# Four-layer network on one core: in the last layer, the three units that issue two pairs of projection pieces move one unit forward

## The chip, the core and the metric

The kernel runs on one core of a Trainium2 chip. The metric is device time in microseconds of one execution. TensorE (PE) multiplies matrices, VectorE (DVE) and GpSimd (POOL) work element by element, ScalarE (ACT) evaluates functions and copies, SyncE (SP) issues most DMAs. Each engine takes its own instructions strictly in order, so a wait at the head of a queue holds everything behind it.

## The reference, cut to what matters

Four layers run one after the other on a tensor of 2 x 192 x 96 x 96. Each is `x = x + layer(groupnorm(x))`. Only the fourth is touched, a selective state-space scan (Mamba) over the 9216 places of an image:

```python
xz = x_flat @ W_in.T                      # 192 -> 768, split into x_in and z_gate
xc = causal depthwise convolution of x_in, 4 taps, + conv_b
x_conv = silu(xc)
x_dbl = einsum('bdl,kd->blk', x_conv, W_x)   # dt (12), B (16), C (16)
delta = softplus(dt @ W_dt.T + 2 * b_dt)
h = exp(delta * A) * h + (delta * x_conv) * B    # 384 channels x 16 states, step by step
y = (h . C + D * x_conv) * silu(z_gate)
out = y @ W_out.T
```

## The kernel before, in words

**Steps and units.** `layer3` cuts the two images into 38 steps of up to 511 places (two short ones of 265 and 264 at the start and at the end). The 6144 pairs of channel and state of a step lie in 12 units, q = 0 to 11, of 4 x 128 rows. A unit k does this:

- PE spreads delta over the rows into four banks of PSUM (`steps_of`, L2466), ACT takes their exponential in place (`decay`, L2480), POOL multiplies the loaded input by B (`times_b`, L2456, tile `bu`), DVE runs four scans (`scan`, L2489, tile `h`).
- DVE multiplies three quarters of h by C (`times_c`, L2513, tile `hc`), POOL the last quarter (`times_c_aside`, L2524, tile `hp`), and PE sums over the states (`sum_of`, L2537, tile `acc`; every fourth unit begins with the skip term, L2531). Every fourth unit DVE gates the sum (`gate`, L2550, tile `y`).
- SP loads the `bu` tile of unit k + 3 (L2441, 1 MB), into one of four buffers.

**Pieces beside the units.** Three generators are run piece by piece between the units' own instructions. `output` (L2562, L2570) projects the finished step before this one. `late` (L2380 to L2430) makes delta for the next step; its last pieces are three POOL operations, `ln`, `dl` and `du` (L2421, L2423, L2425), and four DMAs that write `du` out as `ud` (L2427), from which the `bu` loads of the next step read. `early` prepares the step after the next. After two pieces on ACT (copy of the tail, normalization `xn`) it yields after each of these:

- six projections, P0 to P5: two matmuls on PE (L2344), then one copy on ACT, into `xi` for P0 to P2 (L2352; after P2 also a small copy of the tail, L2354) and into `zs` for P3 to P5 (L2359);
- three convolutions, C0 to C2: four matmuls on PE (L2364), then one bias operation on ACT into `us` (L2368);
- the two silu operations on ACT (L2370, L2371).

The PE half and the ACT half are separate pieces: one call of `go("early")` issues one half. All of these results, and those of `late` and `output`, go through one bank of PSUM, `pe`, which exists once: a projection's first matmul waits until the ACT half of the pair before it has read the bank.

**Who orders what.** PE, ACT, DVE and POOL follow the program order written by hand (`manual_schedule`); SP is not in that list, so the order of its DMAs is the planner's. Within unit k the program order of what matters here is: the pair of `AHEAD[q]`, both halves at once; `sum_of(k - 2)`; `scan(k)`; `steps_of(k + 1)`; the PE half of the pair of `BEHIND[q]`; `decay(k + 1)`; the ACT half of that pair; `times_c(k)`; the gate; the POOL operations; two small ACT copies (`start_of`, L2449, and `keep`, L2496). An AHEAD pair thus stands on PE ahead of the unit's sums and of the next unit's spreading, and its ACT half ahead of the next unit's exponentials; a BEHIND pair stands behind both.

Before the change the pairs of `early` are issued as follows (A for AHEAD, B for BEHIND):

| unit q | 5 | 6 | 7 | 8 | 9 | 10 |
|---|---|---|---|---|---|---|
| pairs | P0 (B) | P1 (B) | P2 (A), P3 (B) | P4 (A), P5 (B) | C0 (A), C1 (B) | C2 (B) |

Of the kernel before, what the change touches and what calls it, by code (L numbers as in the profile page):

```python
# [63 lines left out]
class Net:  # L64
# [2113 lines left out]
    def layer3(self, x, out, stats):  # L2178
# [13 lines left out]
        with ExitStack() as ctx:  # L2192
# [283 lines left out]
            def decay(k):  # L2476
                s, q, _, _ = where(k)
                for r in range(4):
                    da = got[s]["da", q][r][:, 1:]
                    nc.scalar.activation(  # L2480
                        da, da, AF.Exp, scale=nA[:, 4 * q + r : 4 * q + r + 1]
                    )
# [103 lines left out]
            rows_c(0)  # L2586
            steps_of(0)
            decay(0)
            AHEAD = {1: "late", 7: "early", 8: "early", 9: "early"}
            BEHIND = {  # L2590
                0: "late",
                1: "late",
# [12 lines left out]
            def go(name):  # L2605
                next(running[name], None)

            for k in range(nk):
# [5 lines left out]
                if q == 3 and s + 2 < ns:  # L2614
                    running["early"] = early(s + 2)
                if q in AHEAD:
                    go(AHEAD[q])
                    go(AHEAD[q])
                if k >= 2:
# [137 lines left out]
```

## Time and profile before

| | |
|---|---|
| median of 3 runs | 10140.82 us (10130.94 to 10147.6) |
| the profiled execution's own time | 10135.06 us |
| its span, first to last instruction | 10133.3 us |
| scans of the last layer | 7009.5 to 10122.1 us of the span |
| a full step of the last layer | 85.0 us on the mean from scan to scan, twelve units |
| PE / DVE / POOL / ACT busy over the span | 89% / 82% / 69% / 60% |

A full step is read from the timeline: the time from the first scan of one step to the first scan of the next, for steps 3 to 33. Busy shares say little about the order inside a step; the chain of waits and the timeline of one step do. "Granted clock" is the share of full speed that the throttle gave TensorE; its records change at multiples of 3.41 us and hold 1.0 or 0.5. A line such as `7536.29 1.98 PE pe L2344 x4` of the chain view reads: at 7536.29 us of the span the chain lay for 1.98 us on PE, on matmuls of line 2344 writing tile `pe`, four of them (each f32 matmul is recorded as two passes).

### The profile page before, as it was taken

How to read it: one execution, taken by the hardware profiler on the slowest of the kernel's cores; microseconds unless marked ns; L12 is line 12 of the kernel's file. 1: busy time of each engine (PE TensorE's matmuls, PEld its weight loads, DVE VectorE, ACT ScalarE, POOL GpSimd, SP SyncE). 2: the span in 40 equal slices, each digit the busy share in tenths (PEclk: the TensorE clock that was granted, in tenths of full speed). 3: DMA queues.
4: the chain of work that ended last, by engine and by line, in shares of the span. 5: the costliest groups of instructions: out<-in, count | busy, mean ns of one | idle time of the engine just before them, and what ended most of it. 6: DMA issues, size and time to landing. Idle time of an engine off the chain costs nothing. (4 is left out here: it accounts for less than half of the span.)

```text
span 10133.3 us, 222497 instructions
## 1 busy us (share of the span) xinstructions
PE 9017.0 (89%) x87686; PEld 5301.1 (52%) x87686; DVE 8276.5 (82%) x8874; ACT 6078.5 (60%) x11850; POOL 7002.5 (69%) x5653
## 2 busy tenths in 40 slices
PE   4799999999979999999979777787999999999998
PEld 3578878877768877788853222223222222222223
DVE  5788878888768887777756789885899999999998
ACT  0366666666657766677721169664666666666665
POOL 1466676666666666666630258774899999999998
PEclk8899999999989999999989888987999999999998
DMA  8455555555424455455545344443788878788876
GB/s 147 96 135 136 140 135 138 136 136 135 126 72 136 137 144 143 138 137 139 137 117 159 122 141 164 125 128 80 173 178 180 178 178 180 178 178 176 180 177 150
DMA packets 878318, 1465.18 MB, mean 145 GB/s; under 512 B 251745, under 2 KB 682405, under 8 KB 877189
## 3 DMA queue, kind: packets, MB, share of 16 engines
q1 hardware_dynamic: 663276, 1264.09, 49.1%
q0 software_dynamic: 105152, 133.19, 5.7%
q10 hardware_dynamic: 108840, 53.57, 2.1%
q8 instruction: 701, 11.49, 0.5%
q14 instruction: 349, 2.85, 0.1%
HBM read 871.06 MB, written 381.46 MB: 124 GB/s over the span
## 5 line engine op out<-in xcount | busy, mean ns | idle before, releaser
L616 DVE TENSOR_TENSOR sp<-h 128x2304 f32<-128x2304 f32 x790 | 2183.5, 2796 | 34.4 <-ACT h L595 34.4
L2489 DVE TENSOR_TENSOR_SCAN h<-da,bu 128x512 f32<-128x512 f32 (+2 forms) x1824 | 1981.2, 1147 | 239.7 <-ACT da L2480 189.7
L2456 POOL TENSOR_TENSOR bu<-bu,bs 128x2044 f32<-128x2044 f32 (+2 forms) x456 | 1960.0, 4298 | 175.9 <-DMA bu<-ud 127.9
L640 ACT COPY st<-pt 128x512 f32<-128x512 f32 (+1 forms) x2370 | 1214.0, 515 | 1090.0 <-PE pt L632 1017.8
L632 PE MATMUL pt<-ident,sp 128*128 128x128 f32 x14220 | 1677.0, 276 | 84.0 <-DVE sp L616 39.0
L638 DVE COPY st<-pt 128x512 f32<-128x512 f32 x1580 | 1060.3, 687 | 760.2 <-PE pt L632 748.4
L632 PEld LDWEIGHTS pt<-ident,sp 128*128 128x128 f32 x14220 | 1567.9, 142 | 166.1 <-issue 95.5
L586 POOL TENSOR_TENSOR h<-u,step 128x1152 f32<-128x1152 f32 (+1 forms) x474 | 1106.9, 2354 | 628.5 <-DVE u L559 436.9
L604 POOL DMA_DIRECT2D xw<-xp_d x2500 | 1391.0, 619 | 153.9 <-PE pt L683 53.4
L2480 ACT ACTIVATE da<-da,nA 128x511 f32<-128x511 f32 (+2 forms) x1824 | 1063.6, 639 | 583.2 <-PE da L2466 577.2
L683 PE MATMUL pt<-st,xw 64*32 64x288 f32 (+1 forms) x30000 | 1107.7, 370 | 169.1 <-DVE st L638 92.1
L709 ACT COPY val<-pt 128x288 f32<-128x288 f32 (+1 forms) x3000 | 958.7, 404 | 306.3 <-PE pt L683 285.6
L811 PEld LDWEIGHTS pf<-main,wd 126*64 126x64 f32 x17064 | 913.9, 140 | 155.6 <-issue 148.4
L811 PE MATMUL pf<-main,wd 126*64 126x128 f32 (+1 forms) x17064 | 986.5, 274 | 9.6 <-DMA far_m<-val 9.2
L2466 PE MATMUL da<-dl,spread 32*128 32x511 f32 (+2 forms) x3648 | 888.2, 650 | 17.5 <-DVE h L2489 17.4
L683 PEld LDWEIGHTS pt<-st,xw 64*32 64x32 f32 x30000 | 547.7, 106 | 594.7 <-DVE st L638 167.6
L2513 DVE TENSOR_TENSOR hc<-h,cc 128x1533 f32<-128x1533 f32 (+2 forms) x456 | 750.7, 1646 | 0.0
L832 PE MATMUL pf<-more,wl 118*64 118x144 f32 (+5 forms) x11592 | 732.9, 277 | 2.5 <-DMA more<-far_l 2.4
L832 PEld LDWEIGHTS pf<-more,wl 118*64 118x64 f32 (+1 forms) x11592 | 665.7, 137 | 69.7 <-issue 62.7
L2466 PEld LDWEIGHTS da<-dl,spread 32*128 32x128 f32 x3648 | 281.2, 194 | 599.7 <-DVE h L2489 370.2
L2524 POOL TENSOR_TENSOR hp<-h,cs 128x511 f32<-128x511 f32 (+2 forms) x456 | 552.7, 1212 | 47.5 <-DVE h L2489 35.6
L2344 PE MATMUL pe<-xn,sb_w_in 96*128 96x511 f32 (+2 forms) x864 | 479.7, 683 | 91.5 <-ACT zs L2359 38.7
(360 smaller groups left out, 13089.2 us busy)
## 6 DMA issues: line engine op xcount, KB each, us to landing
bu<-ud SPq DMA_DIRECT2D x408, 1022.0 KB
main<-val SPq DMA_DIRECT2D x2016, 91.1 KB
far_l<-val SPq DMA_DIRECT2D x288, 324.0 KB
xw<-xp_d POOLq DMA_DIRECT2D x2500, 26.0 KB, 3.1
far_m<-val SPq DMA_DIRECT2D x288, 162.0 KB
half_d<-hv SPq DMA_DIRECT2D x54, 768.0 KB
hv<-half_d SPq DMA_DIRECT2D x54, 768.0 KB
more<-far_l SPq DMA_DIRECT2D x576, 60.8 KB
```

What stands on the lines that cost most here:

```text
L586: nc.gpsimd.tensor_tensor(hs, u[:, :, 8 * KK * l : 8 * KK * l + n].unsqueeze(3).to_broadcast([P, 2, n, WS]), con["step"].unsqueeze(1).unsq ...
L604: nc.gpsimd.dma_start(out=xw[e * WN : (e + 1) * WN, i], in_=xp_d[y : y + WS, x : x + WS, e * CM // 2 : e * CM // 2 + XW],)
L616: nc.vector.tensor_tensor(sp.rearrange("p s (y x) -> p s y x", x=WS), hy.unsqueeze(3).to_broadcast([P, n, WS, WS]), hx.unsqueeze(2).to_bro ...
L632: nc.tensor.transpose(pt[:, q], sp[:, 2 * (q0 + q) : 2 * (q0 + q) + 2].rearrange("p e w -> p (e w)"), self.ident,)
L640: nc.scalar.copy(st[:, q0 : q0 + m], pt[:, :m])
L683: nc.tensor.matmul(to, xw[e * WN : (e + 1) * WN, win, g * CG : g * CG + 32], sts[pair][e * WN : (e + 1) * WN].rearrange("p s (r c) -> p s ...
L811: nc.tensor.matmul(place(cv, m, 2 - t // 3, 2 - t % 3, None, 0), con["wd"][:, cv, t, m * CO : (m + 1) * CO], blocks(took, 1, rows), start= ...
L832: nc.tensor.matmul(place(cv, m, 2 * cv if alone else 1 - cv, 2 - t, h, 1 - alone,), con["wl"][lanes, slot, t, m * CO : (m + 1) * CO], bloc ...
L2456: nc.gpsimd.tensor_tensor(bu, bu, got[s]["bs"].unsqueeze(1).to_broadcast([P, 4, steps[s][2]]), ALU.mult)
L2466: nc.tensor.matmul(das[r][:, 1:], spread[at, v].rearrange("p n e -> p (n e)"), got[s]["dl"][at, i], start=True, stop=True, tile_position=( ...
L2480: nc.scalar.activation(da, da, AF.Exp, scale=nA[:, 4 * q + r : 4 * q + r + 1])
L2489: nc.vector.tensor_tensor_scan(h[:, r], got[s]["da", q][r], bu[:, r], 0.0, ALU.mult, ALU.add)
```

## The change

The three units whose `AHEAD` entry is "early" become q = 6, 7, 8 instead of 7, 8, 9. `BEHIND` stays as it is.

```diff
-            AHEAD = {1: "late", 7: "early", 8: "early", 9: "early"}
+            AHEAD = {1: "late", 6: "early", 7: "early", 8: "early"}
             BEHIND = {
                 0: "late",
                 1: "late",
```

The pairs of `early` come in the same order as before, so the table becomes:

| unit q | 5 | 6 | 7 | 8 | 9 | 10 |
|---|---|---|---|---|---|---|
| pairs | P0 (B) | P1 (A), P2 (B) | P3 (A), P4 (B) | P5 (A), C0 (B) | C1 (B) | C2 (B) |

P1 to P5 and C0 change their place in the queues of PE and ACT; P0, C1, C2 and the silu operations stay where they were. `early` issues one DMA, the load of `xt`, in its first piece at q = 3, which is not moved. No instruction is added or removed.

## The prediction

> **What bounds the kernel now.** I read the slices of the page first, then the chain of waits over one full step, then the timeline and the stretches of the same step. The page says where the last layer lies and that four resources are nearly full in it:
>
> ```profile
> PE   4799999999979999999979777787999999999998
> DVE  5788878888768887777756789885899999999998
> POOL 1466676666666666666630258774899999999998
> PEclk8899999999989999999989888987999999999998
> DMA  8455555555424455455545344443788878788876
> ```
>
> From slice 28 on (the last layer, 3113 us, 38 steps) nothing is idle enough to tell, so the order inside a step decides. The chain of waits of the step that begins at 7485 us, from unit 6's scan being prepared to the end of unit 9:
>
> ```profile
> 7525.85 3.70 PE pe L2344 x4
> 7529.55 1.70 PE acc L2531 x2
> 7531.25 0.99 PE acc L2537 x8
> 7532.25 1.11 PE da L2466 x8
> 7533.35 2.37 ACT da L2480 x4
> 7535.72 0.52 ACT xi L2352
> 7536.25 0.04 issue
> 7536.29 1.98 PE pe L2344 x4
> ...
> 7547.39 2.37 ACT da L2480 x4
> 7549.76 0.53 ACT zs L2359
> 7550.29 0.04 issue
> 7550.33 3.70 PE pe L2364 x8
> 7554.03 0.99 PE acc L2537 x8
> 7555.02 1.07 PE da L2466 x8
> 7556.09 3.63 PE pe L2364 x8
> ```
>
> The reader sees no DVE and no POOL in it: from 7525.85 until the silu operations at 7570.75 this step's chain is PE and ACT. Three times it crosses over: da on PE, four exponentials on ACT (2.37), the ACT copy of the BEHIND pair (0.52), and back to PE for the AHEAD pair, which waited for that copy because bank `pe` exists once. The first crossing leads to P2, the second (7540.37) to P4, the third (7547.39) to C0. P1, P3 and P5 lie under the exponentials and cost the chain nothing. One full crossing unit is 7532.25 to 7539.27 = 7.02 us; DVE needs 6.13 for a unit (the shortest distance of two scans in the timeline).
>
> P0 and the skip take twice the 1.91 and 0.86 us that such work takes later in the chain. The stretches tell why:
>
> ```profile
> 7525.80:7529.60 3.80, 3.75 (x4) 1.15 (x4) 0.50 0.68 186
> 7609.62:7613.04 3.42, 2.75 (x4) 1.17 (x4) 3.42 (x5) 0.66 (x1) 3.42 (x1) 0.50 0.51 131
> 7613.04:7616.45 3.41, 3.41 (x8) 0.87 (x10) 3.41 (x4) 0.77 (x3) 3.41 (x2) 0.50 0.86 223
> ```
>
> The granted clock (the third number from the end) is 0.50 when P0 runs, and so it is in unit 5 of each of the 30 full steps I looked at. In the second row, the same place a step later, PE was busy 2.75 of 3.42 us and the clock stayed at half; after the third, busy throughout, it came back at 7616.45. In the last layer no half-clock stretch of 3.41 us with 0.6 us or more of idle PE ended in a full clock.
>
> **The change part by part.**
>
> P1 moves ahead of unit 6's sums. On PE it now follows P0 directly, and must wait for P0's ACT copy (0.58 us at 7529.64 in the timeline, after P0's last pass at 7529.55) to free the bank: P1 begins at 7530.30, 0.75 us after P0's end. Queued behind it on PE are the skip, the sums and the spreading for unit 7; unit 7's exponentials and scan wait for those. Before, P1 was free. So the chain gains 0.75 + P1. At full clock P1, skip and sums are 1.91 + 0.86 + 0.99 = 3.76 us.
>
> The clock: the 0.75 us hole falls into the 3.41 us stretch that before was solid PE work and brought the clock back (here 7527.70 to 7531.11). With 78% busy it is like the row of 2.75 in 3.42, and I take it that it does not bring it back. Then the next solid stretch begins 0 to 3.41 us after P1's start, and full clock comes 3.41 to 6.82 us after it, 5.12 on the mean. Half of 5.12, 2.56 us of work, is done by then, the other 1.20 follow: da of unit 7 begins 6.32 us after P1's start (bounds 5.46 and 7.17), at 7536.62 instead of 7532.25, that is 4.37 us late (3.51 to 5.22).
>
> C0 leaves the third crossing. After da of unit 7 the chain has two crossings of 7.02 (to P3 and to P5), then 1.07 + 3.70 (C0, now behind the spreading) + 0.99 + 1.07 to C1: 20.87 us, where before 7532.25 to 7556.09 were 23.84. That gives back 2.97 us. From C1 on nothing differs.
>
> Net, with the clock held back: +4.37 - 2.97 = **+1.40 us a step** (+0.54 to +2.25). In 5 of the 30 steps the clock is already back when P0 ends (8.8 to 9.0 us after unit 5's scan); there P1 runs at full speed and the net is 0.75 + 1.91 - 2.97 = -0.31. Mean: 25/30 x 1.40 - 5/30 x 0.31 = +1.12.
>
> Nothing absorbs it on the usual step: unit 12's exponentials, then both silu on ACT, then unit 13's exponentials make the next link, and DVE is idle before unit 13's scan by 1.09 us on the mean, so a late ACT delays it in full. DVE itself is never ahead again: from da of unit 7 it needs about 41.0 us to the scan of unit 13 (1.9 + 7.02 + 7.02 + 6.72 with the gate + 3 x 6.13), ACT 45.1 - 2.97 = 42.1. But in 4 of 29 steps POOL waited so long for its `bu` (DMA, L2441) that unit 11's scan was later than the delayed one would be; those lose nothing: x 0.85, +0.95.
>
> Edits of no cost: the ACT copies of P1 to P5 stay one per unit and side; `start_of(9)` comes at about 20.3 us after unit 5's scan instead of 15.9, and POOL needs it at 22.6 (cover 2.3 us; if gone, `times_b(9)` slips by the rest, and unit 9's scan, due at 32, has still 5 us). The POOL chain from `ln` to `times_b(9)` starts at DVE's L2419 and stays. SP: no DMA moves; the loads of units 13 to 15 wait for scans that are 1 to 4 us later, bounds 0 and 1 us a step, I take 0 as each lands a unit ahead.
>
> Some 33 steps count (36 run `early`, the short ones count half): 33 x 0.95 = 31 us on the profiled execution's own 10135.06: 10166. That execution lies 5.8 us under the median of 10140.82; against the median I predict 10172.
>
> The Trainium skill speaks the other way on the hole: "TensorE: Matmul & The Clock Gate", section "HAM oscillation", names PE idle gaps above about 3.4 us as what costs the clock. By that, 0.75 us would be harmless and each step would go by the -0.31. The row of 2.75 in 3.42 decides for me.
>
> **Rivals.**
>
> *The clock comes back in spite of the hole*, at P0 and P1 of unit 6, so that P1 runs full. It decides if 0.75 us idle of 3.41 suffices. For it: stretches with only 0.2 to 0.3 us of idle did both. Against: the 0.6 us row above. Price: 33 x -0.31 = -10 us, 10131: not slower.
>
> *The planner puts the load of unit 10 ahead of the first `ud` write.* Now SP issues it at 7542.40, behind the write at 7542.01, though its buffer was free at 7532.4; POOL then idles 1.5 to 3.5 us before `times_b(10)`. For it: in the first three steps the order is another. Against: 30 steps alike, and unit 6's scan does not move. If so, unit 11's late POOL goes too, some 0.5 us a step: with the full clock -27 us, 10114.
>
> *POOL and DMA hide more*: unit 11's scan waits 0.3 to 0.5 us behind `times_b(11)` in the median step; if DMA were later by 1 us, only a third of the delay would show, +10 us, 10151.
>
> *Loads late*: if units 13 to 15 do slip by 1 us, +33 more, 10205.
>
> **How the numbers follow.** This kernel can be told from no change at about 0.2%, 20 us. Forecast (+15 to +63: the bounds of the net x 0.85 x 33): 0.68; clock back: 0.13; planner: 0.05; hidden: 0.08; loads late: 0.06. A little of the forecast lies under +20. Slower 0.70, same 0.22, faster 0.08. The range: from the clock-back case shared over half the steps (10140) to 1.8 us in each of 33 steps (10200).
>
> **What would show it.** Right: in unit 6 P1 takes 3.7 us at clock 0.50; unit 6's scan to unit 7's is about 10 us (6.41 before), unit 9's to unit 10's 6.7 (8.61 before); one crossing fewer in the chain; the full clock some 3 us later than before. Wrong: P1 of 2 us in most steps, a chain through POOL `bu`, or another order of `bu<-ud` and `ud<-du` on SP.

## The result, and the profile after

The kernel after the change took 10205.28 us (median of 4 runs, 10197.38 to 10209.64), beside 10139.06 us of the kernel before: a ratio of 1.0062 (95% interval 1.005 to 1.0073). Beside runs of before in two later sessions it measured 1.0047 (1.0032 to 1.0062) and 1.0050 (1.0037 to 1.0063). It is slower, as forecast, but by some 50 to 66 us where 31 were forecast, and 10205 lies outside the range of 10140 to 10200.

The profiled execution took 10209.64 us (span 10207.7), 74.6 us more than that of before. Of these 16.4 lie in layers that the change does not touch (the scans begin at 7025.9 instead of 7009.5 us; over the profiles of all kernels here, whose earlier layers are the same, they begin anywhere from 7008 to 7043 us, so this part is no effect of the change), and 57.9 in the last layer (3170.6 us from first to last scan instead of 3112.7). A full step is 86.69 us instead of 85.00.

The slices of the page, as shown of before:

```profile
PE   4699999999979999999979777887999999999998
DVE  5688888888767787777765789884899999998998
POOL 1466676666656666666630268774889899899898
PEclk8899999999989999999989788887888888989998
DMA  8455555555424455445544344433777777777776
```

They tell no more than that the layer is stretched. The chain of waits of the same step as before (unit 5's scan now begins at 7546.30 us):

```profile
7551.58 3.76 PE pe L2344 x4
...
7555.42 0.59 ACT xi L2352
7556.01 0.04 issue
7556.06 3.78 PE pe L2344 x4
7559.83 1.58 PE acc L2531 x2
7561.42 0.99 PE acc L2537 x8
7562.41 1.11 PE da L2466 x8
7563.52 2.37 ACT da L2480 x4
...
7573.48 1.98 PE pe L2344 x4
7575.46 0.99 PE acc L2537 x8
7576.46 1.07 PE da L2466 x8
7577.53 3.62 PE pe L2364 x8
7581.15 0.99 PE acc L2537 x8
7582.15 1.07 PE da L2466 x8
7583.22 3.63 PE pe L2364 x8
```

P0, its copy (0.59), then P1 on the chain, both at twice their usual time; C0 (7577.53) now follows the spreading, without an exponential and a copy before it. The stretches of the same place:

```profile
7550.93:7554.35 3.42, 2.77 (x4) 1.17 (x4) 3.42 (x4) 0.66 (x1) 3.42 (x1) 0.50 0.54 133
7554.35:7557.76 3.41, 2.68 (x4) 0.84 (x3) 3.41 (x4) 0.77 (x3) 3.41 (x2) 0.50 0.87 221
7557.76:7561.17 3.41, 3.41 (x5) 1.01 (x3) 2.05 (x2) 0.58 (x1) 3.41 (x3) 0.50 0.28 68
7561.17:7564.60 3.43, 3.43 (x20) 1.15 (x20) 0.34 (x1) 1.10 (x2) 3.43 (x2) 1.00 0.00 0
```

The stretch with the hole (PE busy 2.68 of 3.41 us) does not bring the clock back; the next one, solid, does. So far the profile is as predicted. What was not predicted stands in SP's queue. The DMA issues in the timeline, first of before, then of after, at the same place of the same step:

```profile
7542.40 0.54 SPq L2441 DMA_DIRECT2D bu<-ud  x1
7542.99 1.77 SPq L2427 DMA_DIRECT2D ud<-du  x3
7544.86 10.35 SPq L2441 DMA_DIRECT2D bu<-ud  x2
7555.26 0.61 SPq L2558 DMA_DIRECT2D xr<-x_d  x1
```

```profile
7568.16 0.54 SPq L2441 DMA_DIRECT2D bu<-ud  x1
7568.75 1.88 SPq L2427 DMA_DIRECT2D ud<-du  x3
7570.73 0.54 SPq L2441 DMA_DIRECT2D bu<-ud  x1
7571.31 0.91 SPq L2558 DMA_DIRECT2D xr<-x_d  x1
7580.39 9.81 SPq L2441 DMA_DIRECT2D bu<-ud  x3
```

The load of `xr` (0.4 MB, for the projection of the finished step) stood behind the load of unit 12 and stands now behind that of unit 11, in each of 30 steps: 25 us after unit 5's scan instead of 35. No line of the change names it; SP's order is the planner's, and the planner made another one. All other DMAs of a step keep their order. With that `times_b` of units 11 and 12 begins at 39.3 and 46.0 us after unit 5's scan instead of 38.5 and 44.2. POOL's waits in the same 2600 us, before and after (us in total, times, longest):

```profile
POOL bu L2456 <- DMA bu<-ud: 105.2, 58, 4.3
```

```profile
POOL bu L2456 <- DMA bu<-ud: 142.1, 72, 5.4
```

### The profile page after: what moved, and what is told of

It is laid out like the page before. It is cut to its first block, busy times and chain, and to the rows that moved or that the text cites. A ratio compares the mean times of both kernels' runs of the same rounds, so it can differ in the third digit from the quotient of the medians.

```text
span 10207.7 us, 222499 instructions
## 1 busy us (share of the span) xinstructions
PE 9095.3 (89%) x87686; PEld 5324.4 (52%) x87686; DVE 8261.3 (81%) x8874; ACT 6082.4 (60%) x11850; POOL 6993.8 (69%) x5653
## 5 line engine op out<-in xcount | busy, mean ns | idle before, releaser
L2344 PE MATMUL pe<-xn,sb_w_in 96*128 96x511 f32 (+2 forms) x864 | 542.4, 761 | 116.9 <-ACT xi L2352 64.6
L2524 POOL TENSOR_TENSOR hp<-h,cs 128x511 f32<-128x511 f32 (+2 forms) x456 | 552.6, 1212 | 56.1 <-DVE h L2489 44.2
```

## The experiments

The kernel before took 10139 to 10173 us from one session to another (on one and the same chip 10144 and 10173), so each kernel is told as a ratio to the runs of before made beside it, and step lengths are from one profile each. P0, P1, C0 and the units are named as in the prediction. The diffs are shortened.

**A filler in the hole** (on the kernel after):

```diff
+if q == 6 and s + 2 < ns:
+    fill = decays[(4 * (k + 1)) % 5][:, 1:241]
+    nc.tensor.matmul(fill, taps[:, 0, 0], got[s]["us"][:, 0, :240], start=True, stop=True)
 if q in AHEAD:
```

> The kernel after the change, with one more matmul of 240 columns into a bank that is overwritten next, in the hole between P0 and P1 of unit 6. Theory (the hole of 0.75 us keeps the clock at half through P1, skip and sums): the clock comes back 8.8 to 12.1 us after unit 5's scan, P1 takes 2 to 3 us instead of 3.7, da of unit 7 begins at about 14.0 us instead of 16.2, a step is about 2.2 us shorter than the 86.7 of after: 10130 us (10120 to 10150). Rival (the cost is P1 itself on the chain, and the clock comes back when it likes): no gain, 10205 to 10210 us.

Measured: 1.0044 (1.0031 to 1.0057), 86.33 us a step. Neither the theory's number nor the rival's. In 7 of 30 steps the clock came back 9.5 to 10.2 us after unit 5's scan, and there da of unit 7 began from 13.8 us on; in the other 23 it came at 13.7 to 15.8 us, as in the kernel after (13.7 to 17.1). Those 7 steps show what the hole does: their half-clock stretch ends at 9.5 to 10.2 us and is busy throughout, and each ended in a full clock. In the kernel after, four steps have a stretch that ends at the same place, with 0.58 to 0.73 us of it idle, and none did. The timeline of one of the 23 and the middle one of its half-clock stretches:

```profile
7795.10 3.75 PE L2344 MATMUL pe<-xn,sb_w_in 96*128 96x511 f32 x4 [0.67 <-DVE xr L2570]
7798.64 1.01 PE L2618 MATMUL da<-us,taps 128*128 128x240 f32 x2
7799.58 3.77 PE L2344 MATMUL pe<-xn,sb_w_in 96*128 96x511 f32 x4
```

```profile
7797.88:7801.30 3.42, 3.42 (x6) 1.42 (x5) 3.42 (x4) 0.78 (x3) 3.42 (x2) 0.50 0.87 224
```

By the records PE is busy throughout and the clock stays at 0.50. What kept it there is not shown. P1's first two passes start 1.01 us apart where its others start 0.85 apart, so some 0.15 us may be lost between filler and P1, inside that stretch, and in the 7 steps the stretch ended less than 0.2 us after P1's recorded start. But in the next run stretches with two spacings of 0.99 us did bring the clock back (7 of its 30 steps, 12.6 to 12.8 us after unit 5's scan), so such a loss alone does not explain it.

**The hole alone** (on the kernel before):

```diff
+if q == 6 and s + 2 < ns:
+    mark = ps.tile([P, TM], F32, name="pe")[:, :8]
+    nc.tensor.matmul(mark, taps[:, 0, 0], got[s]["us"][:, 0, :8], start=True, stop=True)
 if q in AHEAD:
```

> The kernel before the change, with one more matmul of 8 columns into the one bank pe ahead of unit 6's sums: it must wait for P0's copy, so it makes the hole, but moves no projection. Theory (the hole holds the clock back): skip, sums, da of unit 7 and P1 run at half clock until 13 to 17 us after unit 5's scan, unit 7's scan comes about 2.9 us late, a step about 87.9 us instead of 85.0: 10235 us (10215 to 10250). Rival (a hole of that size costs only itself): 1.0 us a step, 10172 us.

Measured: 1.0094 (1.0081 to 1.0107), 10237 us, 87.62 us a step, the number that the theory gave. But here too the planner had moved the load of `xr` as in the kernel after, which, as the runs below show, costs 0.3 to 0.5%; so the time alone does not decide. The chain does:

```profile
7557.26 0.60 PE pe L2618 x2
7557.86 1.91 PE acc L2531 x2
7559.77 1.86 PE acc L2537 x8
7561.63 2.05 PE da L2466 x8
```

Skip, sums and spreading take 1.91, 1.86 and 2.05 us where the kernel before needs 0.86 to 1.70, 0.99 and 1.11. The clock came back after 12.6 to 16.0 us (8.8 to 12.2 in before), and da of unit 7 began at 13.77 us instead of 11.59: the 0.75 us hole, with the small matmul that makes it (0.60 us on the chain), costs 2.2 us there.

**One crossing fewer without the hole** (on the kernel before):

```diff
-AHEAD = {1: "late", 7: "early", 8: "early", 9: "early"}
+AHEAD = {1: "late", 7: "early", 8: "early"}
 BEHIND = { ...
+    11: "early",
```

> The kernel before the change, with two double units (7 and 8) and the last pair C2 behind unit 11 instead of a third double unit: no hole, and one crossing from PE to ACT and back fewer. Theory (the crossing at C0 costs 2.97 us of the chain, and it is the hole that ate this gain in the change): a step 0.8 to 1.4 us shorter than 85.0, as far as POOL and DMA let it: 10103 us (10085 to 10120). Rival (unit 11's scan waits for POOL's bu anyway, and the silu comes 2 us later): 10139 to 10170 us.

Measured: 1.0028 (1.0016 to 1.0039), 86.48 us a step: my theory fell. C2 in unit 11 makes `us` and with it both silu later, and unit 12's period grew from 7.29 to 9.43 us; and unit 11's scan came later than unit 10's by 8.03 instead of 7.13, started by POOL's `bu` in 29 of 30 steps.

**AHEAD behind the sums** (on the kernel after):

```diff
-if q in AHEAD: go(AHEAD[q]); go(AHEAD[q])
 if k >= 2: sum_of(k - 2)
+if q in AHEAD: go(AHEAD[q]); go(AHEAD[q])
```

> The kernel after the change, with the AHEAD pair issued behind the unit's sums instead of ahead of them (also late's pair in unit 1): skip and sums of unit 6 cover P0's copy, so PE has no hole, and the sums of units 7 and 8 lie under the wait for the copy. Theory: clock back as in the kernel before, da of unit 7 at about 13.5 us instead of 16.2, each crossing 6.1 instead of 7.0 us, a step of about 84 us: 10105 us (10090 to 10130). Rival (POOL and DMA set unit 11 and nothing below the time of before can come): 10130 to 10150 us.

Measured: 1.003 (1.0018 to 1.0042), 86.33 us a step. On PE it did what was expected: clock back after 9.0 to 12.2 us, da of unit 7 at 13.64 us (16.23 in after), the two crossing units 6.13 and 6.27 us (7.02 and 7.03). Then unit 11's scan was started by POOL's `bu` in 27 of 30 steps and unit 12's in 22: the gain ran into the loads. This was the sign that SP's queue matters.

**The load of xr tied late.** The planner's order was tied by an order edge from the load of unit 5 of the next step to the load of `xr`:

```diff
+with tc.issue_after(loads[-2]):
     nc.sync.dma_start(out=xr, in_=halves(x[b])[:, :, t0 : t0 + T])
```

On the kernel after:

> The kernel after the change, with SP's order tied by hand in one place: the load of xr (L2558), which the planner had put behind the load of unit 11 (25 us after unit 5's scan; before the change it stood behind the load of unit 12, at 35 us), waits in the queue until the load of unit 5 of the next step. Theory (xr's 0.4 MB among the late loads holds back the bu of units 11 and 12, and took the slack that was to absorb some of the delay): unit 11's and 12's scans wait for POOL in fewer steps, 0.3 us a step: 10195 us (10185 to 10202). Rival (from unit 7 on PE and ACT end last in every step, so the planner's order costs nothing here): 10205 us within 5.

On the run with AHEAD behind the sums:

> The run with the AHEAD pair behind the sums, with the load of xr tied late as in the run beside it. Theory (there PE and ACT no longer end last, and what holds it at 86.3 us a step is POOL waiting for the loads of units 11 and 12, which xr delays by 1 to 2 us): a step of 84.3 to 85 us, 10110 us (10090 to 10130). Rival (the loads of units 10 and 11, queued behind the ud writes, set it whatever xr does): 10150 to 10170 us.

On the kernel before:

> The kernel before the change, with the load of xr tied late. Theory (some 0.4 us of a step is POOL's waiting for late loads): 10125 us (10112 to 10135). Rival (no effect while PE and ACT end last): 10140 us within 7.

Measured: 1.0024 (1.0015 to 1.0033) for the kernel after, more gain than the 10 us expected; 0.997 (0.9958 to 0.9982) behind the sums, 85.03 us a step instead of 86.33, though unit 11 still waited for POOL in every step, so half theory, half rival; 0.9994 (0.9985 to 1.0003) for the kernel before, where the rival was right.

**The ud writes tied too**, behind the load of unit 10, on the run with AHEAD behind the sums and xr late:

```diff
+with tc.issue_after(loads[-1]):
     nc.sync.dma_start(out=ud[...], in_=du[32 * r : 32 * r + 32])
```

> The run with the AHEAD pair behind the sums and xr tied late, and the four ud writes (L2427) tied behind the load of unit 10, so that this load goes out at about 12 us after unit 5's scan instead of 21.9. Theory (POOL's waits before units 10 and 11, 1.5 to 5.7 us, come from that place in SP's queue): they go, a step of 81 to 83 us: 10040 us (10010 to 10080). Rival (the 16 DMA engines themselves are full in that stretch, so the place in the queue is indifferent): no more than 10 us below the run without the tie.

Measured: 10046.67 us, 0.988 of before (0.9865 to 0.9895), 81.96 us a step. It beats both kernels. POOL's waits in the same 2600 us, first of the run without this tie, then with it:

```profile
POOL bu L2458 <- DMA bu<-ud: 124.7, 49, 7.1
POOL bu L2463 <- DMA bu<-ud: 37.6, 28, 4.8
```

37.6 us instead of 124.7 (105.2 in before); the load of unit 10 goes out at 11.9 us after unit 5's scan instead of 21.8. The loads of units 10 and 11 had been late by their place in SP's queue, behind writes that wait for POOL's own `du`, and not because the DMA engines were full.

**Both ties alone.** On the kernel before, and on the kernel after:

> The kernel before the change with both ties: xr's load late, the ud writes behind the load of unit 10. Theory (without late loads PE and ACT still end last, at three crossings, so the ties alone give little): a step of 84.5 to 85 us, 0.996 of before (0.994 to 0.999). Rival (the ties are the whole of the 1.2% that the best run gained): 82 us a step, 0.988.

> The kernel after the change with both ties. Theory (the loss is the hole, on PE and ACT, and has nothing to do with loads): a step 1.4 to 1.7 us longer than in the run of the kernel before with the same ties, so about 86.2 us, 1.004 of before (1.002 to 1.006). Rival (the loss came by late loads): within 0.3 us a step of that run.

Measured: 1.0002 (0.9993 to 1.0011) and 1.0018 (1.001 to 1.0027); 85.33 and 85.58 us a step. The ties alone give nothing, so the 1.2% needs both halves. The difference of the two, 0.25 us a step, is below the 1.4 to 1.7 expected and by its letter within the rival's 0.3; by the times it is 0.16%, 13 us, some 0.4 us a step. But the loss on PE is still there: da of unit 7 comes at 15.91 us in the second run and at 12.17 in the first. The clock is a likely reason for the rest, though no run isolates it: all 31 steps of the first run are between 85.04 and 85.67 us long, and their mean is 25 times the 3.413 us of the clock's stretches; of the second run's, 26 are between 85.08 and 85.73. In the first run the clock comes back at 11.8 us in most steps, late in the 8.8 to 12.2 of before, so it sits at a bad place of the stretches (da of unit 7 at 12.17 instead of 11.59), and the other at a good one (15.91 instead of 16.23).

**Which units are double, with everything else mended:**

```diff
 # ties and AHEAD behind the sums, as in the best run
-AHEAD = {1: "late", 6: "early", 7: "early", 8: "early"}
+AHEAD = {1: "late", 7: "early", 8: "early", 9: "early"}
```

> Both ties, the AHEAD pair behind the sums, and the double units at 7, 8 and 9 as in the kernel before the change. Theory (with the sums under the wait for the copy, a crossing costs 6.05 us, less than DVE needs, so it matters little which units are double; DVE and POOL's chain to unit 9 bound both): 81.4 to 82.2 us a step, as the run with units 6 to 8 (81.96): 0.987 of before (0.985 to 0.989). Rival (C0 ahead of unit 9 still costs its third crossing): 83 to 84 us, 0.992.

Measured: 0.9982 (0.9973 to 0.9991), 84.42 us a step; the theory fell, and the rival (83 to 84 us) was nearer on the step but missed the time. Unit 8's period is 8.70 us, where the best run has 6.23: C0 ahead of unit 9 is too long for a crossing. With the hole closed and the loads early, moving the double units forward is worth 2.5 us a step. The change as made has the right direction in the wrong surroundings.

**The place of xr alone, both ways, on one chip.** The load of `xr` is issued in unit 8 behind the load of unit 11, or in unit 9 behind that of unit 12:

```diff
 load(k + 3)
+if q == 8:      # 9 in the second kernel
+    residual(s) # xr's load, with tc.issue_after(loads[-1])
```

The kernel before with the new place; the kernel after with the old place; the kernel after unaltered:

> The kernel before the change, in all queues as it was but for SP: the load of xr goes out behind the load of unit 11, as the planner placed it after the change. Theory (the place costs by itself: the loads of units 11 and 12 land later, POOL waits): 0.3 to 0.6 us a step, 1.002 of before (1.001 to 1.003). Rival (it costs only in company with the longer chain on PE): 1.000 within 0.001.

> The kernel after the change with the load of xr behind the load of unit 12, as before the change: what the change does by PE and ACT alone. Theory (the half clock and the lost crossing leave 0.8 to 1.3 us a step): 1.003 of before (1.002 to 1.004), a third to a half less than the kernel after the change. Rival (all of it is PE and ACT): 1.0055 as the kernel after the change.

> The kernel after the change, unaltered, beside these two: 1.0055 of before (1.0045 to 1.0065) by every theory.

Measured: 1.0049 (1.0036 to 1.0062), more than the theory said, 1.0020 (1.0011 to 1.0029) and 1.0050 (1.0037 to 1.0063). In the traces SP's order is that of the kernel after in the first, and that of the kernel before in the second. POOL's waits of the three, in the same order:

```profile
POOL bu L2458 <- DMA bu<-ud: 157.3, 73, 7.4
```

```profile
POOL bu L2458 <- DMA bu<-ud: 118.2, 57, 6.5
```

```profile
POOL bu L2456 <- DMA bu<-ud: 158.2, 72, 5.7
```

In the kernel before, the new place alone makes `times_b` of units 11 and 12 begin at 39.9 and 46.6 us instead of 38.5 and 44.2, and costs as much as the whole change (0.49%). In the kernel after, the old place takes 0.30% away. The two causes do not add: with `xr` early, the longer chain on PE and ACT costs next to nothing more, because POOL's late `bu` and the late scan of unit 7 delay the same scans of units 11 and 12: in the first of the three POOL's `bu` starts these scans in 24 and 21 of 30 steps, in the third, where they come late anyway, in 7 and 8.

The unaltered kernel after, in another session on another chip:

> The kernel after the change, unaltered, beside the three others on their chip: 1.006 of before (1.005 to 1.007) by every theory; a step of 86.7 us. It tells how much a step of the last layer varies from one profile to the next, and what the run with xr tied late really gained (86.25 us a step).

Measured: 1.0047 (1.0032 to 1.0062), a little under what was expected, and 87.03 us a step. With the 86.69 of the first profile and 87.15 of the last, a step of one kernel varies by some 0.5 us between profiles, so a difference of step length below that says little.

## Why the prediction was wrong, by its steps

- **P1 behind a hole, at half clock: right, and somewhat larger.** P1 took 3.78 us in unit 6, da of unit 7 came 4.64 us later on the mean (16.23 instead of 11.59) where 4.37 was said, inside the bounds of 3.51 to 5.22. Five stretches that began 0.03 to 0.25 us after P1's recorded start, and are busy throughout by the records, still left the clock at half, so it came back from 13.7 us on, not from 13.2.
- **"In 5 of the 30 steps the clock is already back": wrong.** In none of 30. There P0's end used to be followed by the skip at once; now PE was idle for the last 0.07 to 0.46 us of such a stretch (four steps).
- **C0's crossing gives back 2.97 us: right.** From 4.64 us late at da of units 7 to 9 to 1.60 at da of unit 10: 3.04.
- **The periods: right.** Unit 6 to 7 took 10.84 us (about 10 was said), unit 9 to 10 6.73.
- **"x 0.85", POOL's late steps absorb some of it: not as sized.** In the kernel after nothing was absorbed: 1.60 us late at da of unit 10, and the step 1.69 longer, with `times_b` of unit 11 itself 0.8 us later than before. With the old place of `xr`, da of unit 10 was 1.34 us late against the profile of before, but the time says only some 0.7 us a step (0.3 to 0.9): about half was absorbed.
- **"SP: no DMA moves": the step that failed.** The program order of the DMAs did not change, but the planner's order did. The rival on the planner looked at another DMA (the load of unit 10 before the first `ud` write) and only at a gain, and dismissed a change because 30 steps were alike, which says nothing of another program. The moved load of `xr` cost what the forecast had put at nothing: 0.30% in the runs on one chip (1.0050 with it, 1.0020 without), some 30 us.
- **The rival "Loads late" has the measured number, 10205, by luck.** It looked to the loads of units 13 to 15; in 30 steps of the kernel after POOL did not wait for these at all (8.3 us in before). It waited longer for those of units 10 to 12 (140 us instead of 99).

With SP's order held as before (the kernel after with the old place of `xr`) the change costs 0.20%, 0.11 to 0.29, that is 11 to 30 us of the 10173 us of before there; the 31 us forecast are just above it. Two other pairs with one order of SP on both sides differ by 30 us (both with `xr` tied late) and 13 us (both ties). That the forecast comes so near is in part luck: too many favourable steps in it (5 of 30, there were none) and too little absorption work against each other. The kernel after measured 0.50% in the same runs. Counted in this order, of some 51 us about 20 came by the hole and the clock and about 30 by the moved load. Counted the other way, the moved load alone costs all of it (1.0049) and the longer chain next to nothing on top, so the division holds for this order only. The first comparison's 66 us have no such division.

The rule of the Trainium skill weighed in the prediction ("TensorE: Matmul & The Clock Gate", "HAM oscillation", idle gaps above about 3.4 us) is one for losing a full clock. It does not bear on this place, where the clock is at half when P0 runs and has yet to come back: there the row of 2.68 busy us of 3.41 in the profile after shows that a hole of 0.75 us costs another stretch.

## What to carry to other kernels

Where only some queues are ordered by hand, an edit of those changes the planner's order of the others: compare all queues of the two programs, SP's too, before any step is called unmoved. A producer and a consumer through a single PSUM bank leave a hole on PE (here 0.75 us) unless other ready work is put between them; with both ties in place, the same move gained behind such work (0.988) and lost in front of it (1.0018). A DMA that waits for a late engine holds back every load queued behind it (here that of unit 10, by 10 us): tie it behind the loads that are already free to go. That paid only where the loads were what the step waited for; on the kernel before it gave nothing (1.0002).

## What was not expected of the hardware

- Between P0 and the sums of unit 6, little idle time in a stretch of 3.41 us kept the clock at half: in the kernel after no stretch with 0.07 us or more of it there ended in a full clock, and in the run with the hole alone 3.32 busy us of 3.41 did not suffice, 3.38 did. It is no rule for the whole kernel: in that run one stretch elsewhere, 2.76 of 3.41 us busy (7607.87 to 7611.28), did bring the clock back, and with the filler stretches busy throughout by the records did not in 23 of 30 steps. What decides there stays open.
- With the late loads gone, the step locked to the clock's stretches: 31 steps of 85.04 to 85.67 us, on the mean 85.33 = 25 x 3.413, and the clock came back at 11.8 us after unit 5's scan in most of them. An edit of a few tenths of a microsecond could then vanish or count double; no run here tries that.
